# Multi-query attention block on one core: query products 1 and 5 split a second time, a pair of head blocks per PSUM chain, and the steps of a cycle written as two lists

## The chip, the cores and the metric

One Trainium2 chip, one of its cores. The metric is the device time of one execution in microseconds. The profile is one such execution, recorded by the hardware profiler. TensorE multiplies matrices and writes PSUM; VectorE (DVE), ScalarE (ACT) and GpSimd (POOL) do elementwise work, POOL not on PSUM; the DMAs of the main loop are issued by SyncE (SP). Each engine takes its instructions in order and waits on semaphores for the others.

## The reference

x has 64 sequences of 128 tokens and 512 features, all fp32. The core of what is computed:

```python
xn = layernorm(x, g_in)
q = (xn @ Wq).reshape(b, n, H, DH).transpose(0, 2, 1, 3) * scale     # H = 16, DH = 64
kv = xn @ Wkv                                                         # one k and one v for all heads
k, v = (kv[..., :DH], kv[..., DH:])          # with one null key and value put in front
sim = jnp.einsum('bhid,bjd->bhij', q, k) + bias
sim = jnp.where(causal_mask, neg, sim)
sim = jnp.where(mask_p[:, None, None, :], sim, neg)
attn = jax.nn.softmax(sim, axis=-1)
out = jnp.einsum('bhij,bjd->bhid', attn, v)
out = out.transpose(0, 2, 1, 3).reshape(b, n, INNER) @ Wo             # INNER = 1024 -> 512
x = x + layernorm(out, g_out)
```

## The kernel before, in words

**Groups and cycles.** Four sequences make a group (512 tokens), two make a pair, and the main loop, `for c in range(1, B // 2 - 2)`, has 29 calls of `cycle(c)`, one per pair. A cycle works at several depths of a pipeline at once: softmax of the pair `b0 = 2c`, output projection of the pair before it, layer norm and store of the pair before that, queries and scores of the next pair and the next group, and loads far ahead. Prologue and tail are written out by hand.

**Order.** The schedule is manual: the order of the calls in `cycle` is the order of the instructions on every engine. TensorE's order is thus a fixed line: query products, output products and key/value products mixed, and at the end of the cycle `region`, which holds the score products of the next pair (64 matmul calls, four small ones side by side in the array) and the value products of this pair (56 calls). VectorE adds the scores onto the bias (`scores_add`), takes maxima (`scores_max`), transposes the probabilities (`blocks_T`); ScalarE takes the exponentials (`exps`), GpSimd scales by the reciprocal sums (`scale`) and prepares bias and mask (`bias_add`).

**Fast products.** The query projection of a group, 512 features by 512 tokens to 1024 outputs, is done with Winograd's form of Strassen's method: seven half-size products (1 to 7) and sums of blocks. Products 1, 6 and 7 run up in one PSUM bank ("a"), which is copied out after each; product 5 has bank "c" and is added in afterwards. Sums of tokens (`token_sum`, on GpSimd) and sums of weights are made beforehand. `q_one(c, k, h)` does product k for one block of 128 outputs; a cycle does h = 0 and 1, so each product is four matmul calls of 128x128 weights by 256 token columns (two blocks by two halves of the depth).

**Leaves.** From cycle 2 on (`LEAF = 2`) products 2, 3 and 4 are split once more in the same manner: `leaf(c, k, stage)` does one of them for both blocks of the cycle in seven calls of 128 columns. Its sums of tokens come from `leaf_sums` (GpSimd), its sums of weights from `leaf_weights`. After each of its four stages VectorE adds what stands in PSUM onto the query tile `qT` in SBUF.

**The alignment step.** `nc.tensor.addr_align(256, offset=...)` stands once in every cycle (line 1224) and at four places of the prologue (lines 1417, 1429, 1438, 1450). It makes the next TensorE instruction stand at a place that is `offset` modulo 256 in TensorE's instruction stream; the places between are filled. In the cycles the offset is 94, with 120 in cycle 1 and 76 in the last.

**Lines of before that the prediction uses**: 553 and 556 `leaf` (matmul, add), 597 `product`, 358 `kv_mm`, 860 `out_product`, 651 `heads` (scores), 770 `values_one`, 503 the copy of bank "a" into `qT`, 1012 and 1016 the adds of bank "c" (`q_one` with k = 8), 687 `scores_add`, 534 `leaf_sums`, 322 a copy of 512 columns, 1224 the alignment step, 1300 `keep_busy` (matmuls at the very start).

Of the kernel before, what the change touches and what calls it, by code (L numbers as in the profile page):

```python
# [17 lines left out]
def kernel(  # L18
# [63 lines left out]
    P = 128  # L82
# [173 lines left out]
    ident = const.tile([P, P], FP, name="ident")  # L256
# [14 lines left out]
    sp = ctx.enter_context(tc.tile_pool(name="sp", bufs=2))  # L271
    bp = ctx.enter_context(tc.tile_pool(name="bp", bufs=2))
    hp = ctx.enter_context(tc.tile_pool(name="hp", bufs=2))
    small = ctx.enter_context(tc.tile_pool(name="small", bufs=4))
# [7 lines left out]
    def norm_stats(m):  # L282
# [5 lines left out]
        nc.vector.tensor_scalar(rstd, mv[:, 1:2], EPS, None, ALU.add)  # L288
        nc.gpsimd.tensor_tensor(rstd, rstd, nhalf, ALU.pow)
        stats[m] = mv, rstd  # L290
# [35 lines left out]
    def tokens_T(m):  # L326

        g, t = divmod(m, GB)
        if t == 0:
            xbs[g] = hp.tile([P, NQ, KC, NQ, Q], FP, tag="xb", name=f"xb_{g}", bufs=1)  # L330
# [49 lines left out]

    def values_send(g):

        vt = hp.tile([P, NQ, GB, Q], FP, tag="vt", name=f"vt_{g}", bufs=1)
        nc.vector.transpose(vt[DH:], kT[g][DH:])
# [10 lines left out]
    def values_fetch(g):  # L395
        vr[g] = hp.tile([P, NQ, GB, DH], FP, tag="vr", name=f"vr_{g}")
# [98 lines left out]
    wL = const.tile([P, 3, 3, FH, P], FP, name="wL")  # L495
    LEAVES = 2, 4, 3
    xL, leaves = {}, {}
# [4 lines left out]
    def first_into(g, c, h):  # L502
        nc.scalar.copy(q_part(g, c, h), by_block("a"))  # L503

    def leaf_blocks(k):

        w = {2: a12, 4: a22, 3: s4}[k].rearrange("p k (f r m) -> p k r f m", r=2, m=P)
        return w[:, 0, 0], w[:, 1, 0], w[:, 0, 1], w[:, 1, 1]

    def leaf_weights(k, j):  # L510
# [9 lines left out]
        nc.gpsimd.tensor_tensor(o, p, m, op)  # L520

    def leaf_tokens(g, k):
        b = xS[g, 4] if k == 4 else xT[g][:, 0:GH, hi_k] if k == 2 else xT[g][:, GH:, hi_k]
        return b[:, 0, 0], b[:, 1, 0], b[:, 0, 1], b[:, 1, 1]

    def leaf_sums(g, k):

        n = 4 if k == 3 else 3
        xL[g, k] = gp.tile([P, n, N], FP, tag=f"xL{k}", name=f"xL{k}_{g}", bufs=1)
# [3 lines left out]
        for o, p, m in ((t1, b12, b11), (t3, b22, b12), (t2, b22, t1), (t4, b21, t2)):  # L533
            nc.gpsimd.tensor_tensor(o, p, m, ALU.subtract)

    def leaf(c, k, stage):
# [4 lines left out]
        if stage == 0:  # L541
# [5 lines left out]
        t1, t2, t3 = (xL[g, k][:, i] for i in range(3))  # L547
        if k == 3:
            t4 = xL[g, k][:, 3]
# [14 lines left out]
        if stage == 0:  # L564
            mm(pX, w11, b11, True)
            onto(out[:, 0, 0], one(pX))
        elif stage == 1:
# [3 lines left out]
            onto(out[:, 0], two(leaves[k][:, 0:3:2]))  # L571
            onto(out[:, 1, 1], one(pY))
        elif stage == 2:
            mm(pX, w21, t3)
            mm(pY, v4, b22)
            onto(out[:, :, 1], two(leaves[k][:, 1:3]))
        else:
            mm(pX, w22, t4)
            onto(out[:, 1, 0], one(pX))
# [26 lines left out]
    def keep(tag, name):  # L606
        kept[name] = bp.tile([P, HT], FP, tag=f"k{name}", name=f"k{name}", bufs=1)
        nc.scalar.copy(kept[name], prod[tag])

# [79 lines left out]
    def scores_max(b, hf):  # L689
        if hf == 0:  # L690
# [5 lines left out]
    def exps(b, hf, lo=0, hi=R8):  # L696
        if hf == 0 and lo == 0:
# [229 lines left out]
    def pair_norm(b):  # L927
        nmr, rstd = nmrs.pop(b)
        if b % 2 == 0:
# [50 lines left out]
    def q_one(c, k, h):  # L980
        i = 2 * c + 4 + h
        g, f = divmod(i, GB)
        if g >= NG:
            return
        if k == 1 and f % FH == 0:
            q_tile(g, f // FH)
        if k == 1:
            product(g, f, 1, ps_q, "a")
            if c >= LEAF:
                first_into(g, f, 0)  # L990
            else:
                keep("a", "p1")
# [5 lines left out]
        elif k == 6:  # L998
            product(g, f, 6, ps_q, "a", start=False)
            if c >= LEAF:  # L1000
                first_into(g, f, 1)
            else:
                keep("a", "u2")
        elif k == 7:
            product(g, f, 7, ps_q, "a", start=False)
            if c >= LEAF:
                first_into(g, HC + f, 0)
            else:
                keep("a", "u3")
                q_out(g, HC + f, hi_t, "c", "u3")  # L1010
        elif k == 8:
            nc.vector.tensor_tensor(
                q_part(g, HC + f, 1), by_block("c"), q_part(g, HC + f, 0), ALU.add
            )
            o = q_part(g, f, 1)
            nc.vector.tensor_tensor(o, by_block("c"), o, ALU.add)
# [6 lines left out]

    def out_one(p, k, dve=False):
        if not 0 <= p < B:
            return
        if k == 1:
            out_product(p, 1, ps_y, "X")
            out_keep("yp1", 1, dve)
        elif k == 2:  # L1030
            out_product(p, 2, ps_w, "w")
            out_part(p, 0, "w", "yp1")
        elif k == 6:
            out_product(p, 6, ps_y, "X", start=False)
            out_keep("yu2", 2, dve)
        elif k == 5:
            out_product(p, 5, ps_y, "Y")
        elif k == 7:
            out_product(p, 7, ps_y, "X", start=False)
            out_keep("yu3", 1, dve)  # L1040
            out_part(p + 1, 1, "Y", "yu3")
        elif k == 4 and at_end:
            out_product(p, 4, ps_w, "w")
            out_part(p + 1, 0, "w", "yu3")
        elif k == 3 and at_end:
            out_part(p, 1, "Y", "yu2")
            out_product(p, 3, ps_w, "w")
            o = y_half(p, 1)
            nc.vector.tensor_tensor(o, prod["yw"], o, ALU.add)
        elif k == 3:  # L1050
            out_product(p, 3, ps_y, "Y", start=False)
            out_part(p, 1, "Y", "yu2")
        else:
            out_product(p, 4, ps_y, "X", start=False)
            out_last(p + 1)

    def region(c):
# [7 lines left out]
        if n0 < B:  # L1065
            scores_add(n0, 1)
            scores_add(n0, 0)
            if c < 0:
                scores_max(n0, 0)
                scores_max(n0, 1)  # L1070
            scores_add(n1, 0)
            scores_add(n1, 1)
# [4 lines left out]

    def cycle(c):
        b0, b1, n0, n1 = (2 * c + i for i in range(4))
        p, r, m = b0 - 2, b0 - 4, b0 + 10  # L1080
        soft, nxt = b0 < B, n0 < B
        pair, fin, toks = 0 <= p < B, 0 <= r < B, m < B
        first, more = c % 2 == 0, 2 * c + 4 < B
        fetch, send = (b0 + 5) // GB, (b0 + 7) // GB
        if not first and fetch + 1 < NG:
            load_mask(fetch + 1)
        if first and LEAF <= c and more:
            token_sum(c // 2 + 1, 1)
            token_sum(c // 2 + 1, 3)
            token_sum(c // 2 + 1, 2)  # L1090
        if fin:
            pair_stats(r)
        if c == 1:
            load_x(m)
        if pair:
            values_out(p, (0, 2))
        if soft:
            scores_max(b1, 0)
            scores_max(b1, 1)
        if pair:  # L1100
            values_out(p + 1, (0,))
        early = c < LEAF or p < 0
        if not early:
            q_one(c, 1, 0)
        if pair:
            values_out(p + 1, (2,))
        if fin:
            pair_pow(r)
        if soft:
            scores_max(b0, 0)  # L1110
        if c == 1:
            tokens_in(2)
        if first and LEAF <= c and more:
            leaf_sums(c // 2 + 1, 3)
        if early:
            q_one(c, 1, 0)
        if fin:
            pair_nmr(r)
# [531 lines left out]
```

## Time and profile before

| | |
|---|---|
| median of 3 runs | 1023.56 us (1023.29 to 1024.02) |
| profiled execution | 1023.2 us, span 1021.4 us |
| TensorE busy | 1008.8 us, 99% of the span |
| VectorE, GpSimd, ScalarE busy | 852.9, 790.9, 643.1 us |
| mean granted TensorE clock | 0.998 |
| one cycle of the main loop | 30.90 us (from 502.96 to 533.86) |

A row of a group of instructions reads: line, engine, operation, output and input tile, shape, count, then busy time in us and the mean of one in ns, then idle time of the engine ahead of them and what ended it. A row of the time line reads: start, length, engine, line, operation, tile, shape, count. A row for one source line gives, after the engine and operation, the count, the shortest, median and longest duration in ns, and the first and last start in us; PEldq there is the sequencer that feeds TensorE. A matmul's duration is its way through the array; matmuls overlap, so what one costs is the distance of two starts.

### The profile page before, as it was taken

How to read it: one execution, taken by the hardware profiler on the slowest of the kernel's cores; microseconds unless marked ns; L12 is line 12 of the kernel's file. 1: busy time of each engine (PE TensorE's matmuls, PEld its weight loads, DVE VectorE, ACT ScalarE, POOL GpSimd, SP SyncE). 2: the span in 40 equal slices, each digit the busy share in tenths (PEclk: the TensorE clock that was granted, in tenths of full speed). 3: DMA queues.
4: the chain of work that ended last, by engine and by line, in shares of the span. 5: the costliest groups of instructions: out<-in, count | busy, mean ns of one | idle time of the engine just before them, and what ended most of it. 6: DMA issues, size and time to landing. Idle time of an engine off the chain costs nothing. (4 is left out here: it accounts for less than half of the span.)

```text
span 1021.4 us, 31818 instructions
## 1 busy us (share of the span) xinstructions
PE 1008.8 (99%) x12104; PEld 897.8 (88%) x12104; DVE 852.9 (84%) x2000; ACT 643.1 (63%) x2742; POOL 790.9 (77%) x710
## 2 busy tenths in 40 slices
PE   9999999999999999999999999999999999999997
PEld 8888888889888889888899888889888898888876
DVE  6776888988888898888888889888888988878798
ACT  2655776556775556775557765557765557755591
POOL 3799959688696878959689596887968789596874
PEclk9999999999999999999999999999999999999999
DMA  6541351523415153241623506244151522402202
GB/s 216 163 130 51 105 120 38 162 64 116 126 38 153 54 149 94 89 119 37 178 65 105 138 23 159 64 124 118 45 154 46 164 79 83 117 14 64 85 2 104
DMA packets 70264, 100.91 MB, mean 99 GB/s; under 512 B 27744, under 2 KB 31328, under 8 KB 68320
## 3 DMA queue, kind: packets, MB, share of 16 engines
q1 hardware_dynamic: 69008, 97.83, 33.7%
q8 instruction: 96, 1.57, 0.7%
q10 hardware_dynamic: 1104, 1.05, 0.3%
q14 instruction: 56, 0.46, 0.2%
HBM read 63.19 MB, written 33.55 MB: 95 GB/s over the span
## 5 line engine op out<-in xcount | busy, mean ns | idle before, releaser
L701 ACT ACTIVATE s<-s,nmax 128x65 f32<-128x65 f32 (+1 forms) x1024 | 379.2, 409 | 3.5 <-DVE nmax L692 3.5
L701 ACT ACTIVATION_READ_ACCUMULATOR s<-s,nmax 128x1 f32 x1024 | 238.0, 232 | 0.0
L722 POOL TENSOR_TENSOR s<-s,rinv 128x1024 f32<-128x1024 f32 (+1 forms) x128 | 189.7, 1483 | 45.6 <-DVE rinv L718 45.4
L635 POOL TENSOR_TENSOR s<-biasp,mneg 128x1552 f32<-128x1552 f32 x64 | 205.1, 3225 | 2.6 <-DVE biasp L248 2.0
L810 ACT ACTIVATE oT<-poX,nv 128x256 f32<-128x256 f32 x58 | 27.5, 475 | 220.0 <-PE poX L770 113.0
L687 DVE TENSOR_TENSOR s<-ps,s 128x256 f32<-128x256 f32 (+2 forms) x224 | 120.1, 606 | 15.7 <-PE ps L651 15.2
L556 DVE TENSOR_TENSOR qT<-pl,qT 128x128 f32<-128x128 f32 (+1 forms) x420 | 122.6, 324 | 2.7 <-PE pl L553 2.3
L860 PE MATMUL pyX<-wo,oT 128*128 128x256 f32 x512 | 121.4, 380 | 0.0
L692 DVE TENSOR_REDUCE nmax<-s 128x8 f32<-128x520 f32 (+1 forms) x128 | 116.5, 950 | 0.1
L860 PE MATMUL pyX<-wT,oT 128*128 128x256 f32 x488 | 115.6, 380 | 0.7 <-POOL oT L843 0.7
L737 DVE STREAM_TRANSPOSE sb<-s 128x1536 f32<-128x1536 f32 x64 | 113.2, 1768 | 0.6 <-POOL s L722 0.6
L860 PEld LDWEIGHTS pyX<-wo,oT 128*128 128x128 f32 x512 | 96.9, 190 | 14.3 <-issue 0.9
L917 POOL TENSOR_TENSOR rstdo<-rstdo,nhalf 128x1 f32<-128x1 f32 x64 | 35.1, 550 | 86.5 <-DVE rstdo L913 86.5
L860 PEld LDWEIGHTS pyX<-wT,oT 128*128 128x128 f32 x488 | 88.3, 190 | 10.9 <-POOL oT L843 1.1
L651 PE MATMUL ps<-kT,qT 64*64 64x128 f32 (+1 forms) x4096 | 93.6, 245 | 0.4 <-issue 0.4
L651 PEld LDWEIGHTS ps<-kT,qT 64*64 64x64 f32 x4096 | 85.5, 134 | 5.5 <-issue 2.1
L770 PE MATMUL pos<-sb,vr 32*64 32x128 f32 (+1 forms) x1792 | 82.1, 321 | 0.3 <-issue 0.3
L843 POOL TENSOR_TENSOR yS<-oT 128x512 f32<-128x512 f32 x32 | 40.8, 1274 | 45.9 <-ACT oT L810 42.4
L770 PE MATMUL poY<-sb,vr 32*64 32x128 f32 x720 | 74.9, 347 | 0.0
L770 PE MATMUL poX<-sb,vr 32*64 32x128 f32 x960 | 74.0, 299 | 0.0
L503 ACT COPY qT<-pa 128x256 f32<-128x256 f32 x168 | 67.8, 404 | 1.1 <-PE pa L597 1.1
L860 PE MATMUL pyw<-wo,oT 128*128 128x256 f32 x280 | 66.4, 380 | 0.5 <-POOL oT L843 0.5
(150 smaller groups left out, 2517.6 us busy)
## 6 DMA issues: line engine op xcount, KB each, us to landing
res<-in_x_dram SPq DMA_DIRECT2D x64, 256.0 KB, 3.0
out_dram<-y SPq DMA_DIRECT2D x58, 256.0 KB, 2.1
x<-in_x_dram SPq DMA_DIRECT2D x224, 64.0 KB, 2.0
xd<-xb SPq DMA_DIRECT2D x14, 1024.0 KB, 4.7
xT<-xd SPq DMA_DIRECT2D x56, 256.0 KB, 5.2
vr<-vd SPq DMA_DIRECT2D x64, 128.0 KB, 5.9
x<-in_x_dram SPq DMA_DIRECT2D x8, 256.0 KB, 4.8
vd<-vt SPq DMA_DIRECT2D x32, 64.0 KB, 2.2
```

Source lines behind the costliest of these rows:

```text
L503: nc.scalar.copy(q_part(g, c, h), by_block("a"))
L556: nc.vector.tensor_tensor(o, p, o, ALU.add)
L635: nc.gpsimd.tensor_tensor(S[b], biasp, mneg[:, t].unsqueeze(1).broadcast_to([P, R8, ROW]), ALU.add,)
L651: nc.tensor.matmul(to[r][i * DH : (i + 1) * DH, f, :], qT[g, f // FH, t // GH][rows, f % FH, t % GH, NQ - 1 - i if hf else i], kT[g][rows, ...
L687: nc.vector.tensor_tensor(sv, ps, sv, ALU.add)
L692: nc.vector.tensor_reduce(nmax[b][:, hf], S[b][:, :, WITH_NULL[hf]], AX.X, ALU.max, negate=True)
L701: nc.scalar.activation(row, row, AF.Exp, bias=nmax[b][:, hf, k : k + 1], accum_out=rsum[b][:, hf, k : k + 1],)
L722: nc.gpsimd.tensor_tensor(sv, sv, rinvs.pop((b, hf)).unsqueeze(2).broadcast_to([P, R8, sv.shape[2]]), ALU.mult,)
L737: nc.vector.transpose(sb.rearrange("p j e q -> p e j q"), S[b][:, :, 1 : ROW - 1].rearrange("p e (j k) -> p e j k", k=Q),)
L770: nc.tensor.matmul(po[s][rows, half], vr[g][quad(s), j, t, :], sb[quad(s), slots, r * NF : (r + 1) * NF, :], start=start, stop=True, skip_ ...
L843: nc.gpsimd.tensor_tensor(o, l, m, op)
L860: nc.tensor.matmul(prod[key], h[:, c, :], w[:, c, :], start=(start and c == 0), stop=(c == HC - 1), skip_group_check=not start,)
```

## The change

Products 1 and 5 are split a second time too (`LEAVES` gets 1 and 5), from cycle 2 on, each in seven calls of 128 columns in place of four of 256. Unlike the leaves, they don't add onto the query tile in SBUF: `split` keeps the four quarters of a product in the four quarters of a PSUM bank. One quarter, `u`, runs up from stage to stage; after each stage ScalarE copies `u` to a small tile (`turn`), and VectorE adds it into the other quarters of the bank. Then products 6 and 7 run up in the same bank "a" for both blocks of the cycle at once (`pair_product`, the same number of calls as before), with one copy of 512 columns for both (`pair_copy`); bank "c" is added in by two adds of 512 columns (`pair_sum`). Their token sums (`token_sum` 1 and 2, `leaf_sums` 1 and 5) are made in the cycle ahead of the group's first.

Cycle 1 is written out as `second()`. It also makes the new weight sums on VectorE, and `leaf_weights(k, 3)` moves there from GpSimd. From cycle 2 on a cycle goes through one of two lists, `EVEN` and `ODD`; matmuls, copies and adds of a product are now separate entries and stand apart from each other, and `region` is divided into the matmuls and four entries `addS`. Moved with it: `values_fetch` from the odd cycle to the front of the even one (with one buffer), key/value products behind the alignment step in the odd cycle, token and bias steps beside the region. The alignment step stays one entry of each list, with an offset worked out from the number of matmul calls behind it in the list (`left`: 33 in `EVEN`, 31 in `ODD`).

To make room, `ident`, the `kept` tiles and the new token sums share one buffer.

```diff
-    wL = const.tile([P, 3, 3, FH, P], FP, name="wL")
-    LEAVES = 2, 4, 3
+    LEAVES = 2, 4, 3, 1, 5
+    wL = const.tile([P, len(LEAVES), 3, FH, P], FP, name="wL")
...
+    def split(c, k, stage, on):
+        g, fp, f = q_pair(c)
+        if g >= NG:
+            return
+        tag = "c" if k == 5 else "a"
+        if stage == 0 and on == "T":
+            if k == 1:
+                q_tile(g, fp)
+            chain[tag] = ps_q.tile([P, FH, GH, N], FP, tag=tag, name=f"p{tag}_{g}_{f}_{k}")
+            turn[k] = bp.tile([P, 1 + k // 5, N], FP, tag=f"turn{k}", name=f"turn{k}_{g}_{f}", bufs=1)
+        bank = chain[tag]
+        c11, c12, u, c22 = bank[:, 0, 0], bank[:, 0, 1], bank[:, 1, 0], bank[:, 1, 1]
...
+        if on == "S":
+            if stage == 3:
+                nc.scalar.copy(q_rows(g, fp, 0, 0), pair_block("a"))
+            else:
+                nc.scalar.copy(turn[k][:, 1] if (k, stage) == (5, 2) else was, u)
+        elif on == "V":
+            if stage == 0:
+                add(c11, c11, was)
+            elif k == 1 and stage == 1:
+                add(was, c22, was)
+                add(c12, c12, was)
+            elif k == 1:
+                add(c22, c22, was)
+            else:
+                add(c22, c12, turn[k][:, 1])
+                add(c12, c12, was)
+        elif stage == 0:
+            mm(u, w11, b11, True)
+            mm(c11, w12, b21)
+            mm(c22 if k == 1 else c12, v1, t1)
+            if k == 1:
+                mm(c12, v4, b22)
+        elif stage == 1:
+            mm(u, v2, t2)
+        elif stage == 2:
+            mm(u, w21, t3)
+        else:
+            mm(u, w22, t4)
+            if k == 5:
+                mm(c12, v4, b22)
+
+    def pair_product(c, k):
+        g, fp, f = q_pair(c)
+        if g >= NG:
+            return
+        w, t = (s2, xS[g, 2]) if k == 6 else (s3, xS[g, 3])
+        for j in range(FH):
+            for kc in range(HK):
+                nc.tensor.matmul(
+                    chain["a"][:, j],
...
+    def pair_copy(c, k):
+        g, fp, f = q_pair(c)
+        nc.scalar.copy(q_rows(g, fp, k - 6, 7 - k), pair_block("a"))
+
+    def pair_sum(c, u):
+        g, fp, f = q_pair(c)
+        nc.vector.tensor_tensor(
+            q_rows(g, fp, u, 1), pair_block("c"), q_rows(g, fp, u, 1 - u), ALU.add
+        )
...
-            nc.tensor.addr_align(256, offset={1: 120, B // 2 - 3: 76}.get(c, 94))
...
+    def second():
...
+        nc.tensor.addr_align(256, offset=120)
...
+    EVEN = (
+        ("mask_load",),
+        ("vout", 0, 2),
+        ("split", 1, 0),
+        ("vout", 1, 1),
+        ("tsum", 4),
+        ("vfetch",),
...
+        ("split", 5, 2),
+        ("prod", 6),
...
+        ("leaf", 2, 2),
...
+        ("out", 6),
...
+        ("osum", 2),
+        ("align",),
+        ("leaf", 3, 0),
...
+    ODD = (
+        ("vout", 0, 2),
+        ("split", 1, 0),
...
+        ("prod", 6),
...
+        ("split", 5, 3),
+        ("pcopy", 6),
+        ("leaf", 2, 2),
...
+        ("prod", 7),
...
+        ("align",),
+        ("leaf", 2, 3),
+        ("kv",),
...
+    def products(name, *args):
+        if name == "leaf":
+            return (1, 3, 2, 1)[args[1]]
+        if name == "split":
+            return ((4, 1, 1, 1), (3, 1, 1, 2))[args[0] // 5][args[1]]
+        return {"out": 4, "kv": 4, "prod": 4}.get(name, 0)
...
+            "vfetch": when(even, lambda: values_fetch(c // 2)),
...
+            "align": lambda: nc.tensor.addr_align(
+                256, offset=94 + 4 * (33 - left) - (18 if c == B // 2 - 3 else 0)
+            ),
...
+        steps = EVEN if even else ODD
+        left = sum(products(*step) for step in steps[steps.index(("align",)) :])
+        for name, *args in steps:
+            do[name](*args)
...
-    for c in range(1, B // 2 - 2):
+    second()
+    for c in range(LEAF, B // 2 - 2):
         cycle(c)
```

More of the change, by code (lines that the diff above doesn't have):

```diff
@@ L1080, in cycle @@
         p, r, m = b0 - 2, b0 - 4, b0 + 10
[L1081 to L1112, printed above, removed]
@@ L1280, in cycle @@
[L1280 to L1293 removed]
+        g, send = c // 2 + 1, (b0 + 7) // GB
+        soft, nxt, fin, toks = b0 < B, n0 < B, r >= 0, m < B
+        even, more = c % 2 == 0, 2 * c + 4 < B
```

840 lines of the change are left out of this document (568 added, 272 removed).

## The prediction

> **What bounds the kernel now.** I read the page's busy line first, then the busy time of each engine over two whole cycles of the main loop, then TensorE's own line of work in order of time.
>
> ```profile
> span 1021.4 us, 31818 instructions
> PE 1008.8 (99%) x12104; PEld 897.8 (88%) x12104; DVE 852.9 (84%) x2000; ACT 643.1 (63%) x2742; POOL 790.9 (77%) x710
> ```
> ```profile
> 472.06:502.96 30.90, 30.90 (x384) 27.71 (x379) 26.36 (x64) 20.17 (x86) 25.96 (x28) 1.00 0.31 98
> 502.96:533.86 30.90, 30.90 (x383) 27.72 (x379) 26.52 (x65) 20.19 (x86) 22.91 (x17) 1.00 0.40 103
> ```
> The columns of the second view are length, busy PE, PEld, DVE, ACT, POOL, granted clock, DMA. A cycle lasts 30.90 us and TensorE is busy in all of it, at clock 1.00; DVE has 4.4 us free, POOL 4.9 to 8.0, ACT 10.7. So a cycle is the sum of what TensorE is given, and anything else counts only when it holds TensorE up.
>
> ```profile
> 511.73 1.89 PE L358 MATMUL pkv<-xT,wkv 128*128 128x256 f32 x8
> ...
> 514.32 0.39 PE L553 MATMUL pl<-xL,wq 128*128 128x128 f32 x2
> 514.54 0.39 PE L553 MATMUL pl<-xT,wL 128*128 128x128 f32 x2
> 514.76 1.89 PE L860 MATMUL pyX<-wT,oT 128*128 128x256 f32 x8
> 516.49 1.03 PE L597 MATMUL pc<-xS,wS 128*128 128x256 f32 x4
> 517.36 0.38 PE L553 MATMUL pl<-xT,wS 128*128 128x128 f32 x2
> 517.58 0.39 PE L553 MATMUL pl<-xT,wq 128*128 128x128 f32 x2
> ```
> Starts follow each other in lockstep. The four calls of `kv_mm` show as x8: each fp32 matmul call is two MATMUL records, and by the page's equal counts (x12104 each) two weight loads: four instructions. Eight records of 256 columns take 514.76 to 516.49, 0.216 us each; two of 128 columns take 517.36 to 517.58, 0.111 each. A call costs 0.432 or 0.222 us.
>
> **Part 1: what the split saves.** Per cycle, products 1 and 5 are 4 calls of 256 columns each (1.73 us); after, 7 calls of 128 (1.55 us). Saved: 2 x 0.175 = 0.35 us a cycle, 9.8 us in the 28 cycles from 2 on. The 128-column calls already run at this pace, though each loads its weights anew, so there is no further charge.
>
> **Part 2: the other engines.**
> ```profile
> L1012 DVE TENSOR_TENSOR qT<-pc,qT 128x256 f32<-128x256 f32 x56 | 23.2, 414 | 0.0
> L556 DVE TENSOR_TENSOR qT<-pl,qT 128x128 f32<-128x128 f32 x252 | 64.1, 272 | 1.7 <-PE pl L553 1.3
> L687 DVE TENSOR_TENSOR s<-ps,s 128x512 f32<-128x512 f32 x64 | 40.9, 680 | 0.0
> L503 ACT COPY qT<-pa 128x256 f32<-128x256 f32 x168 | 67.8, 404 | 1.1 <-PE pa L597 1.1
> L322 ACT COPY xT<-pxT 128x512 f32<-128x512 f32 x8 | 4.6, 586 | 3.0 <-PE pxT L321 2.9
> L534 POOL TENSOR_TENSOR xL<-xT 128x128 f32<-128x128 f32 x56 | 24.4, 457 | 0.0
> ```
> ```profile
> 76.00:106.90 30.90, 30.64 (x357) 26.38 (x356) 19.40 (x40) 18.36 (x83) 28.45 (x26) 1.00 0.17 47
> vr<-vd SPq DMA_DIRECT2D x64, 128.0 KB, 5.9
> PEld pl L553 <- DVE qT L556: 0.2, 1, 0.2
> ```
> DVE loses four 128x256 adds (`q_one` 8, both lines alike) and gets seven 128x128 adds and two of 128x512: 7 x 0.272 + 2 x 0.680 - 4 x 0.414 = +1.6 us, 28.1 in all. ACT loses six copies and gets six of 128x128 (between 0 and 0.404 each) and three of 128x512: at most +1.8, 22.0. POOL gets eight `leaf_sums` operations per two cycles: +3.7, 52.5 of 61. All stay under TensorE's 30.55 us a cycle, which is their cover; without it they would count only by what exceeds it, which is nothing. The eleven `leaf_weights` on DVE fall in cycle 1, 11 x 0.414 = 4.6 us where the third view has 11.5 free (76.00 to 106.90).
>
> The moved DMAs: `values_fetch` goes from the middle of the odd cycle to the front of the even one, with `vr` in one buffer. SP holds it until the `values` matmuls of the odd region are done, just then; queued behind it are `load_x`, `store` and `load_res` of the same cycle, none due for 10 us. It lands in 5.9 us, and its reader, `values`, stands at the end of a 30 us cycle; without that cover it would cost those 5.9 us in every second cycle. `tokens_in` stays last on SP, and its first reader, `kv`, moves later in the odd cycle. Both cost nothing.
>
> New is that ACT and DVE hand a bank back between the stages of `split`: nine waits a cycle (six stages on a copy of `u`, `prod` 6, `prod` 7, the last call of product 5). Behind each waits all of TensorE. The nearest row is the 0.2 us on the `leaf` adds, one wait in 336 stages: between nothing and 9 x 0.2 = 1.8 us a cycle. I take nothing, as 335 of 336 did.
>
> **Part 3: the `addr_align` step, which decides.** It asks that the next TensorE instruction stand at a given place modulo 256; what fills the gap shows in the trace as NOPs on PE's sequencer.
>
> ```profile
> q8 instruction: 96, 1.57, 0.7%
> L1417 PEldq NOP  x30: 13/13/13, 49.0 to 51.3; - x30
> L1429 PEldq NOP  x25: 13/13/13, 51.4 to 53.2; - x25
> L1438 PEldq NOP  x25: 13/13/13, 53.6 to 55.3; - x25
> L1224 PEldq NOP  x23: 13/13/13, 81.5 to 83.1; - x23
> L1224 PEldq NOP  x26: 13/13/13, 111.9 to 113.7; - x26
> L1224 PEldq NOP  x5: 13/13/13, 513.9 to 514.2; - x5
> L1224 PEldq NOP  x8: 13/13/13, 544.8 to 545.3; - x8
> L651 PE MATMUL ps<-kT,qT 64*64 64x128 f32 (+1 forms) x4096 | 93.6, 245 | 0.4 <-issue 0.4
> ```
> How many. Between the steps at L1417 and L1429 lie 8 calls: 40 + 32 = 72, wanted 97, so 25; the row says 25. Between L1429 and L1438, 6 calls: 97 + 24 = 121, wanted 146: 25 again. A steady cycle of before has 69 calls outside the region (16 + 21 + 28 + 4) and the region's 64 score calls (4096 records in 32 regions, two each) and 56 value calls: 189 x 4 = 756 places, 12 short of 768. The rows show 5 and 8; the other 7 and 4 must be separate semaphore waits that take places too. After, 75 calls lie outside the region: 780 places, past 768, so the next fit is 1024. In detail: even to odd, 94 + 4 x (33 + 44) + 480 = 882 = 114 modulo 256, wanted 102; odd to even, 102 + 4 x (31 + 42) + 480 = 874 = 106, wanted 94. Each time 12 too far: 244 places less the waits. With 8 waits (4 to 7 shown, more handovers now) 236 NOPs in each of cycles 3 to 28. In cycle 29 the target is 18 lower: 218. From `second` to cycle 2 the place reached is 120 + 88 + 480 + 168 = 856 = 88, wanted 94: room for 6, which 7 waits overrun; with 8 it wraps to 254 (with 6 or fewer it is nothing).
>
> What one costs.
> ```profile
> 49.64 1.03 PE L597 MATMUL pa<-xS,wq 128*128 128x256 f32 x4
> 51.33 1.10 PE L597 MATMUL pc<-xT,wS 128*128 128x256 f32 x4 [0.67 <-issue]
> ```
> The record is 13 ns long, but 30 of them span 2.3 us, 25 span 1.8 and 1.7, 23 span 1.6: 74 ns from one to the next on average (71 to 79). It is no queue pressure: TensorE ran dry, stood idle 0.67 us, and the NOPs went on at that pace until the last at 51.3, when the matmul started. The Trainium skill, "TensorE: Matmul & The Clock Gate", section "Wait — 56ns, not 53.3ns?", says that MATMUL and LDWEIGHTS are issued straight to the array, and that a MATMUL sent through the sequencer's program instead takes that program about 62 ns. At 62 ns a NOP the sum below would be 1393; the NOP rows show 74, and they decide.
>
> What is hidden. At 513.9 the first NOP is dispatched while the matmul behind the step starts at 517.36: TensorE has 3.46 us queued (18 records). That is the most it has here; the L1417 row had 49.0 to 50.67, 1.67. In the new even list the last 18 records ahead of the step are `out` 6, `leaf` 2 2 and part of `prod` 6: 8 x 0.216 + 4 x 0.111 + 6 x 0.216 = 3.47; in the odd list 3.04. I take 3.25. The stall is then 236 x 0.0736 - 3.25 = 14.1 us a cycle, between 224 x 0.071 - 3.5 = 12.4 and 240 x 0.079 - 1.7 = 17.3.
>
> What the idle stretch does to the clock.
> ```profile
> 1.36 5.83 PE L1300 MATMUL busy<-ident 128*128 128x128 f32 x28 [1.36 <-POOL nhalf L259]
> L1300 PE MATMUL busy<-ident x7: 421/421/421, 4.9 to 6.2; 128*128 128x128 f32 x7
> L1300 PE MATMUL busy<-ident x7: 274/275/421, 6.0 to 6.9; 128*128 128x128 f32 x7
> 1014.00:1015.00 1.00, 0.44 (x3) 0.03 (x1) 0.91 (x2) 0.00 (x0) 0.23 (x1) 1.00 0.08 31
> 1016.00:1017.00 1.00, 0.00 (x0) 0.00 (x0) 0.93 (x5) 0.00 (x0) 0.06 (x1) 0.93 0.65 250
> 1017.00:1018.00 1.00, 0.00 (x0) 0.00 (x0) 0.91 (x2) 0.00 (x0) 0.49 (x1) 0.50 0.00 0
> ```
> The last matmul ends at 1014.44; 2.4 us later the granted clock falls to 0.50. From rest, matmuls of 128 columns take 421 ns from 1.36 to about 6.2 us and 275 after; some 23 of them at 0.21 instead of 0.111 is 2.2 us lost. A stall of 14 us must drop the clock each cycle. From 0 to 2.3; I take 2.2, the only restart shown.
>
> **Sum.** Cycles 3 to 28: 26 x (14.1 + 2.2 - 0.35) = 414.7. Cycle 29: 218 x 0.0736 - 3.04 + 2.2 - 0.35 = 14.9. Cycle 2: 254 x 0.0736 - 3.47 + 2.2 - 0.35 = 17.1. Together +446.7 on the profiled execution's 1023.2 us: 1470. That execution lies 0.4 us below the median of the runs, which changes nothing here. Against so long a cycle every other engine has slack, so no further wait follows the stall.
>
> **Rivals.**
> - The padding is hidden: a long run of NOPs goes at the pace of plain instructions. In the row below, 128 score records and their loads pass in 2.91 us, 11.4 ns each; 236 at that pace are 2.7 us, under the lead of 3.25. Then the time is 1023.2 - 9.8 = 1013, faster. For it: no row shows a gap of over 30 places, and the 5 and 8 NOPs of now cost nothing. Against it: NOPs at 74 ns with TensorE idle. It decides if less than 0.35 us a cycle is exposed. 0.11, and 0.01 for a stall that just eats the gain.
> ```profile
> 528.57 2.91 PE L651 MATMUL ps<-kT,qT 64*64 64x128 f32 x128
> ```
> - The pace is half again that, 17 ns: 236 x 0.017 - 3.25 - 0.35 = +0.41 us in each of 27 cycles, 1034, slower. The Trainium skill, "Runtime: NRT & Kernel Launch", section "Instruction fetch mechanics", has an issue floor of about 20 cycles an instruction, which would come near it; the NOP rows contradict it. 0.03.
> - The clock stays up in the stall: 1470 - 28 x 2.2 = 1408. The end of the trace speaks against it. 0.08.
> - No padding to speak of, but the bank handovers hold TensorE: 1.8 us a cycle, 1013 + 28 x 1.8 = 1063, slower. The one wait of 0.2 us speaks against it. 0.02.
>
> **Numbers.** The forecast has 0.75: 1470. Its own bounds: 1023 + 27 x (12.4 - 0.35) = 1348 with no clock loss and cycle 2 free; 1023 + 28 x (17.3 + 2.3 - 0.35) = 1562 with all at the top, which no likely mix reaches. 1350 to 1525 holds nearly all of it and the clock rival, about 0.8. Slower by over 0.2% (what this kernel's runs can tell from no change): 0.75 + 0.08 + 0.03 + 0.02 = 0.88; within 0.01; faster 0.11.
>
> **What the new profile would show.** NOPs of the `align` step: about 230 per cycle from cycle 3, spaced about 74 ns; TensorE idle some 14 us in front of `leaf` 3 0 (even) and `leaf` 2 3 (odd), put down to issue; granted clock 0.5 in and behind it, records of 421 ns there; cycle about 46.9 us; one more packet of 16 KB a cycle on the instruction queue q8 (now 96 packets of 1.57 MB). The split calls at 0.222 us would prove part 1. I am wrong if the NOPs are few, or many and dispatched faster than shown, or if TensorE's lead at the step is far over 18 records.

## The result, and the profile after

The changed kernel takes 1487.65 us, the kernel before 1023.58 us in the same comparison: a ratio of 1.4532, 95% interval 1.4503 to 1.456. The prediction was 1470, range 1350 to 1525. The execution profiled first was a disturbed one of 3958 us, so the profile read here comes from a further execution of the same kernel, 1488.79 us, beside which the kernel before took 1022.89.

The head of its page, with the line of the instruction queue:

```profile
span 1487.0 us, 39034 instructions
...
PE 1063.7 (72%) x12440; PEld 942.2 (63%) x12440; DVE 918.6 (62%) x2151; ACT 674.1 (45%) x2826; POOL 834.9 (56%) x819
...
PEclk9989779878898789887897879878898789887899
...
q8 instruction: 123, 2.02, 0.6%
```

TensorE was busy for 99% of the span and is now busy for 72%. It issues 336 more matmul records, but the program has 7216 more instructions: the NOPs go from 328 to 6454, 6326 of them at the `align` step of the two lists. The clock line, 9 everywhere before, now dips. The instruction queue brings 27 packets more (96 before).

Busy time by engine over two whole cycles (length, then busy PE, PEld, DVE, ACT, POOL, granted clock, DMA):

```profile
184.40:232.29 47.89, 33.23 (x391) 29.64 (x391) 27.68 (x70) 23.10 (x92) 28.89 (x33) 0.82 0.15 46
232.29:280.27 47.98, 32.69 (x391) 29.15 (x390) 29.11 (x70) 19.48 (x86) 23.16 (x21) 0.86 0.31 85
```

A cycle takes 47.9 us instead of 30.90. No engine has more than 33.2 us of work in it: for some 15 us none of them bounds the cycle. The NOPs at the `align` step (L1670), first of the whole run, then in an odd cycle, then in an even one (count, duration in ns, first and last start):

```profile
L1670 PEldq NOP  x6326: 13/13/13, 154.6 to 1413.8; - x198
L1670 PEldq NOP  x234: 13/13/13, 154.6 to 171.8; - x117
L1670 PEldq NOP  x236: 13/13/13, 201.6 to 218.9; - x118
```

TensorE's line of work around these two steps (start, duration, line, what it computes; in brackets the idle time ahead and what ended it):

```profile
154.63 1.94 PE L711 MATMUL pa<-xS,wq 128*128 128x256 f32 x8
171.87 0.77 PE L573 MATMUL pl<-xT,wq 128*128 128x128 f32 x2 [15.30 <-issue]
172.43 3.62 PE L363 MATMUL pkv<-xT,wkv 128*128 128x256 f32 x8
...
202.45 1.89 PE L980 MATMUL pyX<-wT,oT 128*128 128x256 f32 x8
219.00 0.77 PE L573 MATMUL pl<-xT,wS 128*128 128x128 f32 x2 [14.65 <-issue]
```

The first two in the list of TensorE's waits:

```profile
PE pl L573 <- issue: 403.9, 27, 15.3
PE pos L890 <- DVE s L807: 3.9, 1, 3.9
```

Twenty-seven waits of 404 us in all, put down to "issue": TensorE waited for nothing but its own instruction stream. 404 / 27 is 14.96 us each. The NOPs fill that time: 234 from 154.6 to 171.8 are 17.2 / 233 = 74 ns apart. The granted clock through the odd cycle's gap, one microsecond a row, with the columns as above:

```profile
156.00:157.00 1.00, 0.57 (x3) 0.17 (x1) 1.00 (x1) 1.00 (x4) 1.00 (x3) 1.00 0.75 266
159.00:160.00 1.00, 0.00 (x0) 0.00 (x0) 0.00 (x0) 0.63 (x4) 0.00 (x0) 0.55 0.00 0
171.00:172.00 1.00, 0.13 (x1) 0.16 (x1) 0.00 (x0) 0.00 (x0) 0.00 (x0) 0.50 0.00 0
176.00:177.00 1.00, 1.00 (x7) 0.92 (x6) 0.91 (x2) 0.00 (x0) 0.00 (x0) 0.91 0.00 0
```

The last matmul ends at 156.57, the clock falls at about 159.1, and it comes back at about 176.2, 4.3 us after the restart at 171.87. In between `kv` takes 3.62 us instead of 1.89.

The whole difference, by TensorE's line of work from the first score matmul of one region to that of the next:

| stretch | before | after | difference |
|---|---|---|---|
| cycles 1 and 2 | 63.01 | 73.27 | +10.3 |
| cycles 3 to 28 (26) | 30.92 each | 47.82 each | +439.3 |
| cycle 29 | 30.05 | 45.48 | +15.4 |
| sum | | | +465.0 |

Measured: 1488.79 - 1022.89 = 465.9. So 455 us are the padded cycles and 10 us are something else, in cycles 1 and 2, where the alignment puts in no more NOPs than before (23 in cycle 1, as before, and none in cycle 2). Both are taken up below.

### The profile page after: what moved, and what is told of

Its sections match the earlier page's. It is cut to its first block, busy times and chain, and to the rows that moved or that the text cites. A ratio compares the mean times of both kernels' runs of the same rounds, so it can differ in the third digit from the quotient of the medians.

```text
span 3956.5 us, 39034 instructions
## 1 busy us (share of the span) xinstructions
PE 3781.2 (96%) x12440; PEld 2550.4 (64%) x12440; DVE 924.2 (23%) x2151; ACT 691.2 (17%) x2826; POOL 832.8 (21%) x819
## 5 line engine op out<-in xcount | busy, mean ns | idle before, releaser
L980 PE MATMUL pyX<-wo,oT 128*128 128x256 f32 x512 | 436.0, 1108 | 0.0
L980 PE MATMUL pyX<-wT,oT 128*128 128x256 f32 x488 | 417.5, 1103 | 0.0
L821 ACT ACTIVATE s<-s,nmax 128x129 f32<-128x129 f32 (+1 forms) x1024 | 372.2, 369 | 14.4 <-DVE nmax L812 11.8
L771 PE MATMUL ps<-kT,qT 64*64 64x128 f32 (+1 forms) x4096 | 325.7, 587 | 0.0
L755 POOL TENSOR_TENSOR s<-biasp,mneg 128x1552 f32<-128x1552 f32 x64 | 204.7, 3201 | 358.0 <-DVE sb L857 337.7
L890 PE MATMUL pos<-sb,vr 32*64 32x128 f32 (+1 forms) x1792 | 267.1, 844 | 0.0
L363 PE MATMUL pkv<-xT,wkv 128*128 128x256 f32 x256 | 234.5, 1187 | 0.0
L980 PE MATMUL pyY<-wT,yS 128*128 128x256 f32 x256 | 220.1, 1102 | 0.0
L980 PE MATMUL pyY<-wo,oT 128*128 128x256 f32 x232 | 199.7, 1103 | 0.0
L711 PE MATMUL pa<-xS,wq 128*128 128x256 f32 x224 | 192.8, 1111 | 0.0
L711 PE MATMUL pa<-xS,wS 128*128 128x256 f32 x224 | 192.8, 1102 | 0.0
```

The source lines that it names most:

```text
L363: nc.tensor.matmul(pkv, wkv[:, kc, :], xT[g][:, t : t + 2, kc, :], start=(kc == 0), stop=(kc == KC - 1),)
L711: nc.tensor.matmul(chain["a"][:, j], w[:, kc, (f + j) * P : (f + j + 1) * P], t[:, :, kc, :], start=False, stop=(kc == HK - 1), skip_group ...
L755: nc.gpsimd.tensor_tensor(S[b], biasp, mneg[:, t].unsqueeze(1).broadcast_to([P, R8, ROW]), ALU.add,)
L771: nc.tensor.matmul(to[r][i * DH : (i + 1) * DH, f, :], qT[g, f // FH, t // GH][rows, f % FH, t % GH, NQ - 1 - i if hf else i], kT[g][rows, ...
L821: nc.scalar.activation(row, row, AF.Exp, bias=nmax[b][:, hf, k : k + 1], accum_out=rsum[b][:, hf, k : k + 1],)
L890: nc.tensor.matmul(po[s][rows, half], vr[g][quad(s), j, t, :], sb[quad(s), slots, r * NF : (r + 1) * NF, :], start=start, stop=True, skip_ ...
```

## The experiments

The theory: the NOPs that `addr_align` puts in to reach a place make the loss, through a stall at 74 ns each and through the clock that falls in it; the split itself gains about 0.3 us a cycle. The rivals: the bank handovers inside `split`, or the new order of the steps, cost as much (then taking the NOPs away leaves the loss); and the length of the program, not the idle time, costs (then the same number of NOPs costs the same wherever it stands). A kernel that ran once has no interval.

| run | kernel | us | ratio to before |
|---|---|---|---|
| e1 | after | 1488.79 | |
| e2 | after, no alignment | 1035.05 | 1.0113 [1.0096, 1.013] |
| e3 | before, no alignment in the cycles | 1036.29 | 1.0127 [1.0112, 1.0142] |
| e4 | before, with a long padding | 1290.01 | |
| e5 | after, jump instead of NOPs | 1023.41 | 1.0002 [0.9993, 1.0012] |
| e6 | e2 with `leaf_weights` spread | 1028.90 | 1.0053 [1.0036, 1.007] |
| e7 | e5 with `leaf_weights` spread | 1019.19 | 0.9959 [0.9944, 0.9973] |
| e8 | e2 (the edit left no mark) | 1031.65 | |
| e9 | e7, two `leaf_weights` behind the region | 1015.15 | 0.9919 [0.9905, 0.9932] |
| e10 | after, padding in four parts | 1264.48 | |

**The changed kernel again.** No edit; its rows are those above.

> The changed kernel itself, once more, for a profile at the usual TensorE clock. My theory: some 236 NOPs at the align step of each cycle from 3 on, 74 ns apart, TensorE idle 14 us per cycle there, and about 2 us per cycle lost to a lowered clock behind it; a cycle of about 47 us, 1470 to 1490 us in all. Rival (the handovers of the banks between ScalarE, VectorE and TensorE hold it up): TensorE's idle time is spread over the split stages and put down to ACT and DVE.

Measured: 1488.79. The idle time is not spread over the stages of `split`: in the list of waits above, 404 us stand ahead of the matmul behind the step.

**The alignment taken out, of the changed kernel and of the kernel before.**

```diff
-            "align": lambda: nc.tensor.addr_align(
-                256, offset=94 + 4 * (33 - left) - (18 if c == B // 2 - 3 else 0)
-            ),
+            "align": lambda: None,
```

> The changed kernel with the align step of its two lists taken out (the one in cycle 1 and those of the prologue stay). My theory, the padding is all of the loss: 1013 us (1008 to 1020), that is 9.8 us under the kernel before. Rival, the handovers or the order of the lists cost too: 1025 to 1065 us.

```diff
         if soft:
-            nc.tensor.addr_align(256, offset={1: 120, B // 2 - 3: 76}.get(c, 94))
+            pass
```

> The kernel before with the align step of its cycles taken out, so that the split can be judged without alignment on both sides. If the place of the instructions in their blocks does not matter: 1023.5 us, within 0.3%. If the alignment was worth something: up to 1 us per cycle more, 1030 to 1050 us.

Measured: 1035.05 and 1036.29. One step taken out takes away 454 of the 466 us; the split, the handovers and the new order remain in the kernel and cost nothing like that. As the maker of the loss that rival falls. But 1035.05 lies above the 1008 to 1020 of the theory and inside the range that was written for the rival, so this run alone does not show that the handovers cost nothing. Its trace has the excess in two places: cycles 1 and 2 take 72.98 us, 10.0 more than before, and the rest lies in the regions, as follows.

But the kernel before also loses 13.4 us when its alignment goes, and it holds only small NOP groups. Its cycles, 30.90 us with the alignment, then take 30.90 to 32.15, and all of the excess lies in the region, between the first score matmul and the first product matmul behind the value matmuls. Two regions of this kernel, in TensorE's line of work:

```profile
756.13 2.91 PE L651 MATMUL ps<-kT,qT 64*64 64x128 f32 x128
...
761.10 0.37 PE L770 MATMUL pos<-sb,vr 32*64 32x256 f32 x1
762.09 0.42 PE L770 MATMUL pos<-sb,vr 32*64 32x256 f32 x1 [0.61 <-issue]
...
762.68 0.48 PE L597 MATMUL pa<-xT,wq 128*128 128x256 f32 x1
...
851.67 2.91 PE L651 MATMUL ps<-kT,qT 64*64 64x128 f32 x128
...
856.96 1.13 PE L597 MATMUL pa<-xT,wq 128*128 128x256 f32 x4
```

From 756.13 to 762.68 are 6.55 us, with TensorE waiting 0.61 us for "issue" in the middle of the value matmuls; from 851.67 to 856.96 are 5.29. The scores take 2.91 us in both. Without the alignment the region starts 5 or 8 places earlier each cycle, modulo 256 (as many as there were NOPs), and the excess comes and goes with that. The changed kernel without alignment does the same: regions of 5.29 to 6.29 us. It holds 788 or 790 places a cycle (1024 less the 236 or 234 NOPs), 20 or 22 past a multiple of 256, so that twelve cycles bring a place back to nearly where it was; and regions of 5.29 us come three in a row from 136, 509 and 880 us, twelve cycles apart. In the changed kernel, with NOPs or with a jump, the steady regions all take 5.29 or 5.30, and so do those of the kernel before but for two (5.39 and 5.52) of the last 26. So the step being tested is worth 13 us in the kernel before, and cannot just be dropped. The Trainium skill, "Runtime: NRT & Kernel Launch", section "Instruction fetch mechanics", says that instructions come in blocks of 256 and that the cost of crossing from one to the next is mostly hidden. The dependence on the place modulo 256 agrees with such blocks; the cost, up to 1.26 us where the crossing falls among short matmuls, does not. That it is the crossing itself that costs is inferred: the runs show the dependence on the place.

**The kernel before, with a long padding.** Nothing but the place is changed: in every odd cycle it is moved by half a block.

```diff
-            nc.tensor.addr_align(256, offset={1: 120, B // 2 - 3: 76}.get(c, 94))
+            nc.tensor.addr_align(256, offset={1: 120, B // 2 - 3: 76}.get(c, 94) ^ (128 * (c % 2)))
```

> The kernel before, with the offset of its align step moved by 128 places in every second cycle, so that each cycle gets 133 to 154 NOPs in place of 5 to 26; nothing else changed. My theory: each cycle loses 135 x 0.074 - 3.5 = 6.4 us idle, and about 2.2 us by the clock: 1275 us (1240 to 1300). If the idle stretch does not lower the clock: 1212. Rival, padding of any length is hidden or jumped and the loss is in the split: 1023.

One cycle's NOPs, the line of TensorE's work at a step, and the first of its waits:

```profile
L1224 PEldq NOP  x133: 13/13/13, 321.8 to 331.4; - x133
```
```profile
212.09 0.77 PE L553 MATMUL pl<-xT,wS 128*128 128x128 f32 x2 [6.54 <-issue]
```
```profile
PE pl L553 <- issue: 177.9, 28, 7.8
```

Measured: 1290.01. So the loss is made in the kernel before too, by padding alone. 133 NOPs go at 9.6 / 132 = 73 ns; 177.9 / 28 = 6.35 us stay exposed per cycle, as the lead of 3.46 us that the prediction read in the kernel before makes them. Cycle 1 has its own padding, 151 NOPs, and loses 6.9 us ahead of an output matmul. Cycles 3 to 28 take 40.16 us on average, 9.26 more than 30.90: 6.3 idle at the step, 0.3 in the regions, half of which are now out of place (up to 6.28 us), and some 2.6 that are left for the clock. 29 x 9.26 = 269, and 267 us were lost.

**The same place reached by a jump.** `max_nops=0` makes `addr_align` jump over the gap.

```diff
-                256, offset=94 + 4 * (33 - left) - (18 if c == B // 2 - 3 else 0)
+                256, offset=94 + 4 * (33 - left) - (18 if c == B // 2 - 3 else 0), max_nops=0
```

> The changed kernel with its align step kept, but the padding jumped over by a branch instead of executed (max_nops=0). The region's place in its blocks is then the good one in every cycle. If the branch costs nothing on TensorE's path: 1014 us plus some 10 us of cycle 1, 1024 us. If it costs up to 1 us a cycle: up to 1051 us. If the loss had come from the place and not from the executed NOPs: 1488 us as before.

The jumps, and TensorE's work around the first of them:

```profile
L1670 PEldq COMPARE_BRANCH  x27: 275/292/316, 152.8 to 948.3; - x27
```
```profile
152.84 1.94 PE L711 MATMUL pa<-xS,wq 128*128 128x256 f32 x8
154.62 0.38 PE L573 MATMUL pl<-xT,wq 128*128 128x128 f32 x2
```

Measured: 1023.41, 465 us less than with NOPs, and as fast as before. The gap in the program is the same (the instruction queue still brings 123 packets); a jump of 0.29 us hides under the 1.94 us that TensorE has queued, and 17.3 us of NOPs do not. The steady cycles alternate between 30.57 and 30.62 us, 0.305 less than before, and TensorE has no wait in them. Against that, a padded cycle of 47.82 loses 17.2: 14.96 idle and 2.2 to the clock.

That saves 26 x 0.305 = 7.9 us, and yet the kernel is no faster: cycles 1 and 2 take 71.3 us instead of 63.01. (With the NOPs they took 73.27; there the granted clock also fell to 0.50 at about 80.6 us, behind the first wait of cycle 1, and here it did not.) What is late there shows in the changed kernel's list of waits above, 3.9 us ahead of the value matmuls for `s` from DVE. In the same stretch, DVE's line of work and then POOL's:

```profile
97.86 1.72 DVE L529 TENSOR_TENSOR wS<-wS 128x256 f32<-128x256 f32 x1
99.50 3.43 DVE L529 TENSOR_TENSOR wq<-wq 128x256 f32<-128x256 f32 x1
102.86 0.41 DVE L1005 TENSOR_TENSOR y<-pyY,kyu 128x256 f32<-128x256 f32 x1
...
104.71 2.53 DVE L807 TENSOR_TENSOR s<-ps,s 128x1024 f32<-128x1024 f32 x5
```
```profile
96.09 6.56 POOL L755 TENSOR_TENSOR s<-biasp,mneg 128x1552 f32<-128x1552 f32 x2
102.61 1.30 POOL L554 TENSOR_TENSOR xL<-xT 128x128 f32<-128x128 f32 x2
```

A later cycle of the same run, POOL and then DVE:

```profile
182.07 6.41 POOL L755 TENSOR_TENSOR s<-biasp,mneg 128x1552 f32<-128x1552 f32 x2 [0.56 <-DVE mneg L745]
184.72 0.41 DVE L1005 TENSOR_TENSOR y<-pyY,kyu 128x256 f32<-128x256 f32 x1
```

Two `leaf_weights` sums (L529) of the size that takes 0.41 us elsewhere take 1.72 and 3.43 us. Each ends 0.3 us after the `bias_add` (L755) that was running when it started; the second at 102.93, when POOL's second `bias_add` has ended at 102.65. The addition at L1005, which has one input in PSUM, keeps its 0.41. Here both `bias_add`s are over; but in the later cycle shown, and 16 times in the run, it lies wholly within a `bias_add` and takes 0.38 to 0.42. The five additions of the scores (L807), on which the value matmuls wait, start only at 104.71. The Trainium skill, "SBUF — State Buffer", section "SBUF: two separate sides", says that a DVE operation with two SBUF inputs and a GpSimd operation that reads SBUF take turns on a shared port, and that the loser blocks for the whole of the other's instruction. These rows agree with it: the wait lasts about as long as one `bias_add`, 3.2 us. The first wait of cycle 1, 2.6 us ahead of a product (L622) for DVE in the run with the NOPs, has the same maker: six such sums in a row from 72.8 us, 0.94 to 1.49 us each, beside sums of POOL.

**`leaf_weights` spread over cycle 1.** The block of six in `second()`, and three more later, go between other steps, away from the `bias_add`s; two stay. The edit is the same on the kernel without alignment and on the one with the jump:

```diff
         out_sum(p, 1)
-        for j in (1, 2, 4):
-            leaf_weights(1, j, nc.vector)
-            leaf_weights(5, j, nc.vector)
+        leaf_weights(1, 1, nc.vector)
+        leaf_weights(5, 1, nc.vector)
...
         q_one(1, 3, 0)
+        leaf_weights(1, 2, nc.vector)
+        leaf_weights(5, 2, nc.vector)
...
         q_one(1, 2, 1)
+        leaf_weights(1, 4, nc.vector)
+        leaf_weights(5, 4, nc.vector)
...
         out_one(p, 3)
-        leaf_weights(2, 3, nc.vector)
-        leaf_weights(1, 3, nc.vector)
-        leaf_weights(5, 3, nc.vector)
```

(The last three go to `q_one(1, 6, 1)`, `out_one(p, 6)` and `out_one(p, 7)`.)

> The changed kernel without the align step in its lists (1035 us) and with the eleven leaf_weights of cycle 1 spread over the cycle on VectorE instead of standing in two bunches. Theory: the two bunches hold up TensorE by 2.4 and 3.9 us and let its clock fall, 8 to 10 us in all: 1025 to 1028 us. Rival, those operations cost the same wherever they stand: 1035 us.

> Both at once: padding jumped by a branch, and leaf_weights spread. If both theories hold and the branch is free: 1014 to 1016 us, under the kernel before (1022.9). If the branch costs 0.3 us a cycle or more: no gain on the kernel before.

Measured: 1028.90 and 1019.19, that is 6.2 and 4.2 us less than the kernels they are made from, and above their forecasts (1025 to 1028 and 1014 to 1016). Nine of the eleven sums were moved, not all as the first of the two texts has it. The wait in the region is still there in the second, 3.6 us in the list of waits, and its region takes 10.49 us instead of 5.29. The two `leaf_weights` that had not been moved stand among the `bias_add`s just ahead of it, in DVE's line of work:

```profile
94.48 1.74 DVE L529 TENSOR_TENSOR wS<-wS 128x256 f32<-128x256 f32 x1
96.15 3.42 DVE L529 TENSOR_TENSOR wq<-wq 128x256 f32<-128x256 f32 x1
```

**These two moved behind the region.**

```diff
         bias_add(n0)
-        leaf_weights(3, 3, nc.vector)
...
         q_one(1, 4, 1)
-        leaf_weights(4, 3, nc.vector)
...
         region(1)
+        leaf_weights(3, 3, nc.vector)
+        leaf_weights(4, 3, nc.vector)
```

> As the run with the jumped padding and the spread leaf_weights (1019.2 us), with the last two leaf_weights of cycle 1 (those of leaves 3 and 4) moved behind the region. There they stood beside bias_add on GpSimd, took 1.7 and 3.4 us, and TensorE waited 3.6 us for the score adds behind them. Theory: cycle 1 to 2 goes from 35.8 to about 31 us: 1014 to 1015.5 us. Rival, the two operations only move the wait to the head of cycle 2: 1018 to 1020 us.

The head of its page, the two additions, and the two cycles in which the 10 us lay, then a steady cycle:

```profile
span 1013.4 us, 32735 instructions
...
PE 1001.0 (99%) x12440; PEld 900.8 (89%) x12440; DVE 910.8 (90%) x2151; ACT 674.7 (67%) x2826; POOL 834.7 (82%) x819
```
```profile
L529 DVE TENSOR_TENSOR wS<-wS x1: 581/581/581, 101.2 to 101.2; 128x256 f32<-128x256 f32 x1
L529 DVE TENSOR_TENSOR wq<-wq x1: 672/672/672, 101.7 to 101.7; 128x256 f32<-128x256 f32 x1
```
```profile
63.04:94.45 31.41, 31.41 (x361) 27.21 (x361) 24.29 (x48) 19.64 (x86) 29.30 (x24) 1.00 0.45 121
94.45:126.30 31.85, 31.70 (x391) 28.06 (x390) 27.30 (x67) 21.44 (x89) 31.23 (x37) 1.00 0.15 44
156.92:187.50 30.58, 30.58 (x392) 27.81 (x391) 27.59 (x70) 23.11 (x92) 28.87 (x33) 1.00 0.23 71
```

Measured: 1015.15, ratio 0.9919 [0.9905, 0.9932]: 0.8% faster than the kernel before, with the whole change in it. The two additions take 0.58 and 0.67 us among POOL's short operations, cycles 1 and 2 take 63.26 us, 0.25 more than before, and the region 5.53. In its list of waits TensorE has none over 1.4 us, and none on a DMA. So the 10 us were the two sums beside `bias_add` and the pile ahead of them. Of the 8.6 us gained, 7.9 are the 26 shorter cycles.

**The same padding in four parts.** If the idle time and not the number of NOPs costs, four short gaps must cost less than one long one. A first attempt with 59 plain NOPs at each of four places a cycle failed: none of them stands in the trace, whose 32708 instructions are those of the kernel without alignment.

> The changed kernel without the align step, with the same 236 NOPs a cycle in four parts of 59 at out 2, out 5, the old place and out 7. Theory: each part costs 59 x 0.0737 - lead, with a lead of 1.9 to 2.7 us as in the changed kernel's own profile 1.7 to 2.4 us, four of them 6.8 to 9.6 us a cycle, and the clock stays up since no idle stretch reaches 2.4 us: 1035 + 28 x 6.8 to 9.6 = 1225 to 1304 us. Rival, a NOP costs its 74 ns wherever it stands: 1035 + 28 x 17.4 = 1522 us.

Measured: 1031.65; this run says nothing on the question. It lies 2.0 us under the lowest of the four runs of the kernel without alignment, which has the same number of instructions, so a single run can be that far off. It was made again with four alignments a cycle (behind `out` 2, `out` 5 and `out` 7, and at the old step), each 61 places past the next natural place:

```diff
+        def part():
+            spot[0] = (spot[0] + 4 * spot[1] + 61) % 256
+            spot[1] = 0
+            nc.tensor.addr_align(256, offset=spot[0])
...
-            "align": lambda: nc.tensor.addr_align(
-                256, offset=94 + 4 * (33 - left) - (18 if c == B // 2 - 3 else 0)
-            ),
+            "align": part,
```

> The changed kernel with its align step replaced by four, at out 2, out 5, the old place and out 7, each with an offset 61 places past the natural one, so about 59 NOPs less the waits at each. Theory: a NOP costs 74 ns less what TensorE has queued (1.9 to 2.7 us at the old place): 1.7 to 2.4 us each, four of them 6.8 to 9.6 us a cycle, on top of the 1035 us without the align step, and the clock stays up, since no idle stretch reaches 2.4 us: 1225 to 1304 us. If the queue holds 3.46 us everywhere: 1135 us. Rival, 74 ns a NOP wherever they stand, with nothing hidden: 1035 + 28 x 17.4 = 1522 us.

The NOPs of one cycle, the four gaps in TensorE's work there, and the clock over the same stretch:

```profile
L1628 PEldq NOP  x233: 13/13/13, 307.9 to 332.0; - x117
```
```profile
312.16 0.46 PE L668 MATMUL pc<-xL,wL 128*128 128x128 f32 x2 [1.35 <-DVE rstd L288]
316.81 0.46 PE L668 MATMUL pa<-xT,wq 128*128 128x128 f32 x2 [2.01 <-issue]
326.78 0.46 PE L573 MATMUL pl<-xT,wq 128*128 128x128 f32 x2 [2.49 <-issue]
332.06 0.46 PE L573 MATMUL pl<-xT,wS 128*128 128x128 f32 x2 [1.07 <-DVE nmr L302]
```
```profile
308.00:320.00 12.00, 8.64 (x48) 7.25 (x48) 7.51 (x23) 8.48 (x40) 6.73 (x8) 1.00 0.60 139
320.00:332.00 12.00, 8.50 (x44) 7.02 (x42) 7.66 (x19) 7.65 (x35) 8.53 (x9) 1.00 0.16 47
```

Measured: 1264.48. The number of NOPs is about the same (6581 in all, 233 in this cycle), the loss about half. Of each part some 2 to 3 us stay under what TensorE has queued, so the four gaps here come to 6.9 us instead of 15.

The clock stays at 1.00 in this stretch, but not in the whole run, and there the theory fails. In cycles 3 to 28 no idle stretch is longer than 2.57 us, and yet the granted clock falls to 0.50 in 18 places, for 3.4 us each. In one of them, behind gaps of 1.30 and 2.03 us, an output product takes 3.58 us instead of 1.89:

```profile
394.00:396.00 2.00, 2.00 (x8) 1.64 (x8) 1.03 (x3) 1.69 (x8) 0.00 (x0) 0.59 0.00 0
```

So four short gaps idle less than one long one, and cost less clock (18 short falls instead of 26 long ones), but they do not keep the clock up; the time came out in the range with this part of its reason wrong. The rival that the program's length costs falls: the instruction queue brings 124 packets here, 123 in the changed kernel and 123 with the jump, at 1264, 1488 and 1023 us.

## Why the prediction was right

The forecast of 1470 lies 1.2% under the 1487.65 measured, and the mechanism was the one given. By its steps:

- **How many NOPs.** 236 in each cycle from 3 on were worked out; 234 and 236 stand in the trace. Taking eight semaphore waits was right within two (eight in the even cycles, ten in the odd).
- **What one costs.** 74 ns, in a group of 25 as in a group of 236; 73 in the kernel before with 133. The pace of plain instructions and the 17 ns rival fall, and so does the 62 ns sum: 1393.
- **What is hidden.** 3.25 us was taken, and it is less. In the odd cycle 1.94: only the eight records of `prod` 7 were queued when the NOPs began. ACT's copy of `prod` 6 out of bank `a`, which `prod` 7 must wait for, stands so in ACT's line of work of the changed kernel:

```profile
153.94 0.59 ACT L722 COPY qT<-pa 128x512 f32<-128x512 f32 x1 [0.32 <-PE pa L711]
```

It ends at 154.53, and the first NOP follows at 154.6. So the bank handover that the prediction took at nothing does not idle TensorE, but it holds the sequencer until 0.1 us before `prod` 7 starts, and TensorE goes into the padding with less lead than the 3.04 us worked out for the odd list. In the even cycle it is 2.74 (204.34, the end of `out` 6, less 201.6). There it is VectorE that holds the sequencer: `leaf` 2 2 writes into the tile `pl` that the adds of `leaf` 2 1 still read, and waits for them. They stand so in DVE's line of work:

```profile
200.84 0.61 DVE L576 TENSOR_TENSOR qT<-pl,qT 128x256 f32<-128x256 f32 x2
```

They end at 201.45. In all 27 padded cycles the first NOP follows the copy by 0.07 us (odd) or these adds by 0.11 to 0.15 us (even). The stall came out at 14.96 instead of 14.1: 27 x 0.86 = 23 us.
- **The clock.** 2.2 us lost per restart was taken from the start of the kernel, and 2.2 to 2.3 is what the cycle lengths leave: 47.82 less 30.595 less 14.96. The old trace had shown a fall 2.4 us after the last matmul, and that is no fixed delay: it is 2.5 us in the first two gaps, then 2.1 to 2.3 in the even cycles and 5.1 to 5.4 in the odd ones. In the third gap the last matmul ends at 252.73, and the clock falls at about 258.1 (granted clock 1.00 up to 258, and 0.55 in the microsecond from there). That the one restart at the start of the kernel gave about the right price for all of these is in part luck.
- **The saving of the split.** 0.35 us a cycle predicted, 0.305 measured; the 128-column calls go at 0.22 us.
- **DVE, ACT, POOL, the moved DMAs.** Hidden in the steady cycles: with the jump, cycles of 30.6 us run without a wait on any of them.
- **Cycle 2's padding.** Predicted to wrap round to 254 NOPs and to cost 17.1; there was none, so exactly six places were taken. The text itself set the condition: a room of six places, overrun by seven or more waits. It was read to the wrong side.
- **`leaf_weights` in cycle 1.** Taken as hidden, 11 x 0.414 = 4.6 us in 11.5 free: this step failed. The duration came from an addition with a PSUM input, and these have two SBUF inputs and POOL's long additions beside them. Busy time free over the cycle says nothing of the last few microseconds ahead of a region. It cost most of the 10.3 us of cycles 1 and 2, and with the padding gone it would have made "no change" of a gain.

The terms that were off add up to -17 for cycle 2, +10 for cycles 1 and 2, and +23 for the lead: 16 of the 18 us between forecast and result. That the forecast came within 1.2% is thus in part luck: the -17 takes away half of the +33. All the rivals fall. "The padding is hidden" came nearest to being useful: its 1013 is what the change is worth once the padding is a jump and the eleven sums are out of the way, 1015.15.

## What to carry to other kernels

When an edit changes how many instructions stand between two aligned places, count the places again: a fill just under a block turns into nearly a block, and long fills belong in a jump, not in NOPs. Ask of any work on the issuing side what TensorE has queued at that spot, and look for the wait just ahead, since that set the lead in the changed kernel. For an addition moved to DVE, take the duration from a row with the same kind of inputs, and look at what POOL runs in the same microseconds.

## What the runs showed that was not expected

- A region whose instructions lie badly against the blocks of 256 takes up to 6.55 us instead of 5.29, with TensorE idle for "issue". That is 13.4 us over the kernel before (1036.29 against 1022.89) and 10 to 12 us over the changed one (e2 against e5, e6 against e7), and it is what the alignment step buys.
- A jump over some 240 places costs 0.29 us on TensorE's sequencer, and nothing behind 1.9 us of queued matmuls.
- The same 128x256 addition on DVE, with both inputs in SBUF, takes 0.41 us alone and 3.43 beside a POOL addition; with one input in PSUM it takes 0.38 to 0.42 beside the same POOL addition.
- With the padding in four parts the granted clock fell to 0.50 in 18 places over 26 cycles, though no idle stretch there was longer than 2.57 us.
